# Second attention of a two-layer kernel: products of scores in bursts of three tiles, and a fixed order on TensorE

## Chip, cores and metric

The kernel runs on one core of one Trainium2 chip. The metric is the device time of one execution in microseconds (us); lower is better. One chip core has a matrix engine (TensorE, "PE" in the profile, with its weight loads as "PEld"), a vector engine (VectorE, "DVE"), an activation engine (ScalarE, "ACT"), a general engine (GpSimd, "POOL") and SyncE ("SP"), which starts transfers here. Each engine takes its instructions in the order of its own queue.

## The reference

Two layers, each an attention and a mixture of experts, on 4 sequences of 1024 tokens of 256 numbers in fp32. The change lies in the second attention:

```python
Q = x @ wq + bq                      # x is the normalised input, (4, 1024, 256)
K = x @ wk + bk
V = x @ wv + bv
Q = Q.reshape(B * H, S, D)           # 64 heads of 1024 rows of 16 numbers
...
scores = jnp.einsum('bqd,bkd->bqk', Q, K) / jnp.sqrt(jnp.float32(D))
attn = jax.nn.softmax(scores, axis=-1)
ctx = jnp.einsum('bqk,bkd->bqd', attn, V)
...
out = ctx @ wo + bo
out = out + x
out = (out - mu) * jax.lax.rsqrt(var + LN_EPS) * gamma + beta
```

There is no mask: every one of the 64 heads has a full 1024 x 1024 table of scores. The softmax is computed with the true maximum of each row taken off before the exponential.

## The kernel before

**How the second attention is tiled.** The 64 heads are taken in 32 pairs (`NP`), numbered `p`. One pair of heads gives the 128 rows of one output tile of tokens. The table of scores of a pair is computed twice. First with queries down and keys across (`maxima`, L1368): VectorE reduces each 128 x 1024 tile to row maxima (L1381). Then with keys down and queries across (`scores`, L1407): here two more small products take the row maxima off (the operand `top_st`), and ScalarE writes the exponentials to the tile `pT` (L1424), which the weighted sums (`sums`, L1427) use with the values `v_t` as weights. Both kinds of score tile lie in PSUM under the tag `two`, of which there are three (`psa`, L80). The sums of a pair gather in one PSUM bank, `acc`. Everything else that passes through PSUM there uses one bank, `misc`.

**The loop.** A step `s` stands for one of eight blocks of keys (`KT`) of one pair; it has two halves, so a pair has 16 half-steps and the stage 512. In a half-step the loop (L1605) records, in this order: one tile of `scores` (two products with the keys, L1416, then two with the maxima, L1416), one tile of `maxima` for the pair that comes 12 steps later (`AHEAD`; two products, L1374), one half of the sums of the step before (four products, L1431), and then `some`, which advances the side jobs by one piece. The two products of a kind in a score tile use the two halves of the array's rows, 64 each, one head per half; the four products of the sums use four groups of 32 output columns.

**Side jobs.** `some` (L1567) takes one piece each from `between` and `aside`, and one from `outs`, `projects` or `gating`; `sort` follows when there was little else. They are generators:
- `outs` holds `put_out` (L1442) for a finished pair. Its first piece transposes the copy `oT` of the sums (L1447) and divides (L1452, L1454); later ones transpose again (L1464), project (L1470) and add the residual, in which VectorE's L1477 needs GpSimd's addition of `bo` (L1476).
- `projects` holds `project` (L1269: L1286, and L1296 with two PSUM tiles of tag `two`) and `values` (L1323: L1336), once each for four pairs.
- `between` and `gating` hold the layer norm after the attention (`finish`: L1492 to L1509), and the first steps of the next mixture of experts (L958 to L996).
- `sort` ranks tokens for the experts of the first half of the batch on VectorE, and `aside` then writes those ranks by 16 scatters (L1542) on GpSimd.

When all eight blocks of a pair have their maxima, `max_rows` (L1383) reduces once more, transposes the result on TensorE (L1390), splits it in two parts, and sends it through DRAM into a row buffer of `top_ring` by four transfers on SP (L1398, L1403).

**What sets the order.** The engines' queues are filled by a scheduler at build time. It goes by the recorded order and by its own estimate of when each instruction can start, so it may put a later instruction ahead of an earlier one. `issue_after` forbids this for what is recorded inside it: side jobs are held behind the newest instruction of the main work on their engine, kept in the dictionary `newest`. For TensorE `newest` holds only the last of the sums; score products and the transpose of the tops are free to move.

Of the kernel before, what the change touches and what calls it, by code (L numbers as in the profile page):

```python
# [18 lines left out]
P = 128  # L19
# [4 lines left out]
UT = 4  # L24
UN = UT * P
NU = NT // UT
# [13 lines left out]
def two_layers(  # L40
# [33 lines left out]
    nc = tc.nc  # L74
    mm = nc.tensor.matmul
# [1121 lines left out]
    with ExitStack() as lc:  # L1197
# [68 lines left out]
        halves, vals, normed = {}, {}, {}  # L1266
        newest = {}

        def project(u: int):  # L1269

            xnT = normed[u] = pool.tile([P, 2, UN], F32, tag="xnT", name="xnT_a1", bufs=1)
            for jp in range(UT // 2):
                xns = []
                for i in (u * UT + 2 * jp, u * UT + 2 * jp + 1):
                    xn = work.tile([P, D], F32, tag="xn", name="xn")
                    nc.gpsimd.tensor_scalar(
                        xn, x_t[i], mv_all[:, i, 0:1], rstd_all[:, i : i + 1],
                        ALU.subtract, ALU.mult,
                    )
# [88 lines left out]
        def maxima(p: int, j: int, kk: int, tops):  # L1368

            q_st, k_st = q_ring[p % RING], k_ring[p % RING]  # L1370
            sc = two_banks().rearrange("p (h c) -> p h c", h=2)
            for hh in range(2):
                rows = slice(HR * hh, HR * hh + HR)
                mm(  # L1374
                    sc[:, hh],
                    lhsT=q_st[rows, j * P : (j + 1) * P],
                    rhs=k_st[rows, kk * 512 : (kk + 1) * 512],
                    start=True,
                    stop=True,
                )  # L1380
            newest["vector"] = nc.vector.tensor_reduce(tops[:, :, j, kk], sc, AX.X, ALU.max).ins  # L1381

        def max_rows(p: int, tops):  # L1383

            top = small.tile([P, 2 * 8], F32, tag="top", name="top")
            nc.vector.tensor_reduce(
                top, tops.rearrange("p h j k -> p (h j) k"), AX.X, ALU.max
            )
            ps = misc_bank()
            nc.tensor.transpose(ps[:16, :P], top, ident)  # L1390
            split = pool.tile([16, 2, P], F32R, tag="top_split", name="top_split")
            nc.scalar.copy(split[:, 0, :], ps[:16, :P])
            nc.vector.tensor_tensor(
                split[:, 1, :], ps[:16, :P], split[:, 0, :].bitcast(F32), ALU.subtract
            )
            d = dram.tile([2, 2, S], F32, tag="tops_d", name="tops_d", bufs=3)
            for hh in range(2):
                nc.sync.dma_start(  # L1398
                    out=d[hh].rearrange("n (j q) -> j n q", q=P),
                    in_=split[8 * hh : 8 * hh + 8].bitcast(F32),  # L1400
                )
            for hh in range(2):
                nc.sync.dma_start(  # L1403
                    out=top_ring[p % 2][HR * hh : HR * hh + 2].bitcast(F32), in_=d[hh]
                )

        def scores(p: int, k: int, rp: int):  # L1407


            q_st, k_st = q_ring[p % RING], k_ring[p % RING]  # L1410
            sc = two_banks()
            cols = slice(rp * 512, (rp + 1) * 512)
            for top in range(2):
                for hh in range(2):
                    rows = slice(HR * hh, HR * hh + HR)
                    mm(  # L1416
                        sc[:, hh * 512 : (hh + 1) * 512],
                        lhsT=minus[rows] if top else k_st[rows, k * P : (k + 1) * P],
                        rhs=(top_ring[p % 2] if top else q_st)[rows, cols],
                        start=not top,  # L1420
                        stop=bool(top),
                    )
            pt = pool.tile([P, 1024], F32, tag="pT", name="pT", bufs=6)
            newest["scalar"] = nc.scalar.activation(pt, sc, AF.Exp).ins  # L1424
            return pt

        def sums(p: int, k: int, hh: int, pts, oT_ps):  # L1427

            n = 2 * p + hh
            for r in range(4):  # L1430
                newest["tensor"] = mm(  # L1431
                    oT_ps[32 * r : 32 * r + 32, hh * D : (hh + 1) * D],
                    lhsT=vals[n // HU][:, n % HU, k, :],
                    rhs=pts[r // 2][:, hh * 512 + (r % 2) * D : hh * 512 + (r % 2 + 1) * D],
                    start=(k == 0 and hh == 0),
                    stop=(k == 7),
                    skip_group_check=True,
                ).ins

        ys = []  # L1440

# [109 lines left out]

        AHEAD = 12
        KT = 8
        outs, projects, between, gating, sort, aside = [], [], [], [], [], []
# [20 lines left out]
        def all_of(jobs):  # L1577
            while jobs:
                step(jobs)

        top_parts = {}

        def maxima_step(m: int, kk: int):
            p, j = divmod(m, KT)
# [16 lines left out]
        for m in range(AHEAD):  # L1601
            for kk in range(2):
                maxima_step(m, kk)
        before, oT_ps = None, None
        for s in range(NP * KT + 1):  # L1605
            p, k = divmod(s, KT)
            if k == 0:
                if p % UT == 1:

                    all_of(projects)  # L1610
                    if p // UT + 1 < NU:
                        projects.append(values(p // UT + 1))
                if p + 3 < NP:
                    load(p + 3)
                if p % UT == 3 and p + 5 < NP:
                    all_of(projects)
                    projects.append(project(p // UT + 2))
            if k == 1:
# [10 lines left out]
            if k == 0 and s:  # L1629
# [5 lines left out]
                outs.append(put_out(p - 1, oT))  # L1635
# [102 lines left out]
```

## Time and profile before

| what | us |
|---|---|
| median of 3 runs (2560.59 to 2582.25) | 2569.44 |
| the profiled execution, own time | 2580.51 |
| its span in the trace | 2578.6 |
| TensorE busy (90% of the span) | 2328.3 |
| VectorE busy (54%) | 1396.7 |
| ScalarE busy (38%) | 986.0 |
| GpSimd busy (25%) | 640.4 |
| row maxima L1381, 512 instructions, mean 1.217 | 619.0 |
| exponentials L1424, 512, mean 1.025 | 523.5 |
| weighted sums L1431, 4096 records | 345.0 |
| keys' products L1416, 1024 | 261.2 |
| maxima's products L1374, 1024 | 232.1 |
| subtracted maxima L1416, 1024 | 208.2 |

Busy times are shares of an average over quite different stages; the second attention is one of them. TensorE's records overlap, since products in different parts of the array run side by side and ends are modelled, so its busy time says little about how fast it could go. Distances from start to start in the timeline say more. An fp32 product of the sums leaves two records, so that four products show as eight.

The busy time of each engine in three stretches of the stage (columns: engine, busy us in a window of 100 us):

| window | PE | DVE | ACT | granted clock |
|---|---|---|---|---|
| 1650 to 1750 | 97.47 | 77.78 | 66.86 | 1.00 |
| 1950 to 2050 | 97.48 | 75.58 | 62.79 | 0.98 |
| 2150 to 2250 | 93.59 | 93.52 | 64.82 | 1.00 |

### The profile page before, as it was taken

Reading aid. Unit: us, or ns where it says so; the run is one execution under the profiler, and the core shown is the slowest. Engines: PE = TensorE matmul, PEld = TensorE weight load, DVE = VectorE, ACT = ScalarE, POOL = GpSimd, SP = SyncE. Lnnn points to the kernel's source line nnn. Section 1 sums busy time; section 2 is a strip of 40 time slices with the busy share of each in tenths; the row PEclk is TensorE's granted clock in tenths of the full one; section 3 lists DMA queues with packets and bytes.
Section 4 is the critical chain, followed back from the end, with each engine's and each line's share of the span. In section 5 each row is a group of like instructions: output and inputs, shape, how many; then the busy total and the mean of one; then the engine's idle time right before and its main releaser. Section 6 shows DMA issues by size and latency. Waiting matters only on the chain.

```text
span 2578.6 us, 42321 instructions
## 1 busy us (share of the span) xinstructions
PE 2328.3 (90%) x16882; PEld 1389.6 (54%) x16882; DVE 1396.7 (54%) x2272; ACT 986.0 (38%) x1345; POOL 640.4 (25%) x741
## 2 busy tenths in 40 slices
PE   6999999899999999999957999999999999997534
PEld 3566666566578888885533444444444444443322
DVE  6445445514222222224536777676767798994293
ACT  1333333221122222221112666565656565665311
POOL 2333333601700000004340013122221211124354
PEclk8998999899999999999976999999999999998667
DMA  3000000510266666663143231312131312100134
GB/s 92 17 10 10 10 13 8 166 48 23 104 185 196 194 192 194 194 192 88 51 98 68 52 74 52 67 43 68 43 68 43 67 43 67 43 19 11 54 118 131
DMA packets 202976, 207.52 MB, mean 80 GB/s; under 512 B 89128, under 2 KB 163496, under 8 KB 202780
## 3 DMA queue, kind: packets, MB, share of 16 engines
q1 hardware_dynamic: 179292, 163.37, 23.4%
q0 software_dynamic: 11792, 30.18, 3.9%
q10 hardware_dynamic: 11696, 11.27, 1.3%
q8 instruction: 133, 2.18, 0.4%
q14 instruction: 63, 0.52, 0.1%
HBM read 141.49 MB, written 58.80 MB: 78 GB/s over the span
## 4 chain that ended last, share of the span: by engine, by line
PE 72%; DVE 15%; ACT 4%; issue 4%; DMA 2%; POOL 2%; SPq 0%; POOLq 0%; ACTq 0%; DVEq 0%
PE two L847 10%; PE two L1416 10%; PE acc L1431 8%; PE two L643 7%; DVE tops L1381 6%; PE two L329 5%; PE two L1374 4%; PE acc L871 4%; PE two L258 2%; PE two L1296 2%; PE misc L660 2%; PE acc L660 2%; PE two L321 2%; PE acc L396 1%; DVE glu_b L860 1%
## 5 line engine op out<-in xcount | busy, mean ns | idle before, releaser
L1381 DVE TENSOR_REDUCE tops<-two 128x2 f32<-128x1024 f32 x512 | 619.0, 1217 | 126.7 <-PE two L1374 124.7
L1424 ACT ACTIVATE pT<-two 128x1024 f32<-128x1024 f32 x512 | 523.5, 1025 | 329.1 <-PE two L1416 324.5
L1431 PE MATMUL acc<-pT,v_t 128*32 128x256 f32 x4096 | 345.0, 397 | 5.4 <-ACT pT L1424 5.4
L1416 PE MATMUL two<-q_st,k_st 64*128 64x512 f32 x1024 | 261.2, 503 | 32.2 <-DVE tops L1381 19.7
L847 PE MATMUL two<-xbT,w_t 128*128 128x256 f32 x1248 | 275.8, 379 | 0.7 <-ACT xbT L839 0.7
L847 PEld LDWEIGHTS two<-xbT,w_t 128*128 128x128 f32 x1248 | 237.0, 190 | 33.1 <-ACT xbT L839 0.9
L1374 PE MATMUL two<-k_st,q_st 64*128 64x512 f32 x1024 | 232.1, 421 | 20.1 <-DMA k_st<-halves 9.3
L643 PE MATMUL two<-xnT_f,w_t 128*128 128x512 f32 x512 | 229.8, 601 | 3.1 <-DVE glu L652 3.1
L1416 PEld LDWEIGHTS two<-q_st,k_st 64*128 64x128 f32 x1024 | 97.2, 185 | 225.0 <-issue 127.9
L860 DVE SCALAR_TENSOR_TENSOR glu_b<-two,b_blk,act_b 128x256 f32<-128x256 f32 x156 | 75.3, 483 | 249.4 <-ACT act_b L857 249.4
L1416 PE MATMUL two<-top_st,minus 64*128 64x512 f32 x1024 | 208.2, 401 | 0.0
L857 ACT ACTIVATE act_b<-two,b_blk 128x256 f32<-128x256 f32 x156 | 74.0, 474 | 330.6 <-PE two L847 287.6
L898 POOL DMA_INDIRECT yr<-ys_d,slot x64 | 61.4, 960 | 538.1 <-DMA ys_d<-yb 471.1
L1431 PEld LDWEIGHTS acc<-pT,v_t 128*32 128x32 f32 x4096 | 86.8, 108 | 167.9 <-issue 145.8
L871 PE MATMUL acc<-w_t,glu_b 128*128 128x256 f32 x624 | 161.8, 392 | 6.4
L1374 PEld LDWEIGHTS two<-k_st,q_st 64*128 64x128 f32 x1024 | 107.6, 191 | 92.4 <-DVE tops L1381 28.9
L643 PEld LDWEIGHTS two<-xnT_f,w_t 128*128 128x128 f32 x512 | 96.3, 192 | 111.7 <-issue 105.7
L355 DVE TENSOR_REDUCE top<-two 128x4 f32<-128x768 f32 (+1 forms) x128 | 112.5, 919 | 71.3 <-PE two L329 71.3
L381 POOL TENSOR_SCALAR_AFFINE_SELECT pT<-pT 128x1024 f32<-128x1024 f32 x64 | 70.4, 1100 | 305.5 <-ACT pT L378 305.5
L378 ACT ACTIVATE pT<-two 128x768 f32<-128x768 f32 (+1 forms) x128 | 93.7, 783 | 121.2 <-PE two L329 120.7
L651 ACT ACTIVATE act<-two,bT 128x512 f32<-128x512 f32 x64 | 44.0, 687 | 241.8 <-PE two L643 230.7
L871 PEld LDWEIGHTS acc<-w_t,glu_b 128*128 128x128 f32 x624 | 112.2, 189 | 37.5 <-DVE glu_b L860 25.2
(304 smaller groups left out, 3110.9 us busy)
## 6 DMA issues: line engine op xcount, KB each, us to landing
w_t<-in_L_ffn_rw_dram SPq DMA_DIRECT2D x117, 512.0 KB
halves<-split SPq DMA_DIRECT2D x64, 256.0 KB
q_st<-halves SPq DMA_DIRECT2D x128, 128.0 KB
k_st<-halves SPq DMA_DIRECT2D x256, 64.0 KB
xs_d<-zeros SPq DMA_DIRECT2D x6, 1664.0 KB
xb<-xs_d SPq DMA_DIRECT2D x39, 256.0 KB
ys_d<-yb ACTq DMA_DIRECT2D x39, 256.0 KB
b_t<-in_L_ffn_rb_dram SPq DMA_DIRECT2D x39, 128.0 KB
```

Source lines behind the costliest of these rows:

```text
L329: mm(parts[r][:, gg, :], lhsT=left[32 * r : 32 * r + rows, g, l0 : l0 + P], rhs=right[32 * r : 32 * r + rows, g, r0 : r0 + n], start=(mask ...
L355: nc.vector.tensor_reduce(tops[i][:, 2 * ab : 2 * ab + 2, 2 * gp : 2 * gp + 2], scs[ab], AX.X, ALU.max)
L643: mm(ps[:, n * 512 : (n + 1) * 512], lhsT=w_t[:, kc, f * P : (f + 1) * P], rhs=xnT[:, kc, cols], start=(kc == 0), stop=(kc == 1),)
L660: mm(ps[:, jj * D : (jj + 1) * D], lhsT=glu[:, f, j * P : (j + 1) * P], rhs=w3_t[:, f, :], start=(f == 0), stop=(f == NF - 1),)
L847: mm(ps[:, (2 * m + ff) * BT : (2 * m + ff + 1) * BT], lhsT=w_t[:, kc, f * P : (f + 1) * P], rhs=xbT[:, kc, :], start=(kc == 0), stop=(kc ...
L860: nc.vector.scalar_tensor_tensor(glu[:, f, :], ps[:, (2 + ff) * BT : (3 + ff) * BT], b_blk[1][:, f, n : n + 1], act, ALU.add, ALU.mult,)
L871: mm(ps[:, a * D : (a + 1) * D], lhsT=glu[:, f, a * P : (a + 1) * P], rhs=w3_t[:, f, :], start=(f == 0), stop=(f == NF - 1),)
L1374: mm(sc[:, hh], lhsT=q_st[rows, j * P : (j + 1) * P], rhs=k_st[rows, kk * 512 : (kk + 1) * 512], start=True, stop=True,)
L1381: newest["vector"] = nc.vector.tensor_reduce(tops[:, :, j, kk], sc, AX.X, ALU.max).ins
L1416: mm(sc[:, hh * 512 : (hh + 1) * 512], lhsT=minus[rows] if top else k_st[rows, k * P : (k + 1) * P], rhs=(top_ring[p % 2] if top else q_st ...
L1424: newest["scalar"] = nc.scalar.activation(pt, sc, AF.Exp).ins
L1431: newest["tensor"] = mm(oT_ps[32 * r : 32 * r + 32, hh * D : (hh + 1) * D], lhsT=vals[n // HU][:, n % HU, k, :], rhs=pts[r // 2][:, hh * 5 ...
```

## The change

The loop over steps becomes a loop over half-steps `h`, and the work of a half-step is cut into `weigh` (the score tile whose exponentials are wanted), `seek` (the maxima tile), `add_up` (the sums) and `rest` (side jobs). Three half-steps are recorded together: `weigh`, `seek`, `weigh`, then one half of the sums, then `seek`, `weigh`, `seek`, then two halves of the sums. The last half-step but one of each pair, and the first two of all, stay by themselves. A new function `own` holds every product of scores and sums behind the one recorded before it on TensorE, and the transpose of the tops is held in the same way. `max_rows` is no longer called in the middle of the maxima but from `rest`, after the sums. The sum's copy `oT` and `put_out` now start right after the last sums of a pair, before the pieces of `rest`; before, one `some` came first.

```diff
+        def own(*a, **k):
+            with ExitStack() as behind:
+                if "tensor" in newest:
+                    behind.enter_context(tc.issue_after(newest["tensor"]))
+                newest["tensor"] = mm(*a, **k).ins
...
-                mm(
+                own(
                     sc[:, hh],
...
-            nc.tensor.transpose(ps[:16, :P], top, ident)
+            with ExitStack() as behind:
+                if "tensor" in newest:
+                    behind.enter_context(tc.issue_after(newest["tensor"]))
+                newest["tensor"] = nc.tensor.transpose(ps[:16, :P], top, ident).ins
...
             if j == KT - 1 and kk == 1:
-                max_rows(p, top_parts.pop(p))
+                full.append(p)
...
-            pts = []
-            for half in range(2):
-                if p < NP:
-                    pts.append(scores(p, k, half))
-                    maxima_step(s + AHEAD, half)
-                if s:
-                    sums(*divmod(s - 1, KT), half, before, oT_ps)
-                some(half == 0 and k % 4 == 0)
-            before = pts
...
+        def rest(*hs):
+            while full:
+                p = full.pop(0)
+                max_rows(p, top_parts.pop(p))
+            for h in hs:
+                some(h % 8 == 0)
+        h = 0
+        while h < LAST:
+            if h < 2 or h % (2 * KT) == 2 * KT - 2 or h + 3 > LAST:
+                weigh(h)
+                seek(h)
+                add_up(h)
+                rest(h)
+                h += 1
+            else:
+                weigh(h)
+                seek(h)
+                weigh(h + 1)
+                add_up(h)
+                rest(h)
+                seek(h + 1)
+                weigh(h + 2)
+                seek(h + 2)
+                add_up(h + 1)
+                add_up(h + 2)
+                rest(h + 1, h + 2)
+                h += 3
```

`weigh` also calls `turn` at the first half-step of a pair, which loads the queries and keys of the pair three further on and starts `project` and `values`, as the head of the old step did.

More of the change, by code (lines that the diff above doesn't have):

```diff
@@ L1415, in scores @@
                     rows = slice(HR * hh, HR * hh + HR)
-                    mm(
+                    own(
                         sc[:, hh * 512 : (hh + 1) * 512],
@@ L1430, in sums @@
             for r in range(4):
-                newest["tensor"] = mm(
+                own(
                     oT_ps[32 * r : 32 * r + 32, hh * D : (hh + 1) * D],
@@ L1437, in sums @@
                     skip_group_check=True,
-                ).ins
+                )
         ys = []
@@ L1579, in all_of @@
                 step(jobs)
-        top_parts = {}
+        top_parts, full = {}, []
         def maxima_step(m: int, kk: int):
@@ L1603, in two_layers, with turn, weigh, seek @@
                 maxima_step(m, kk)
[L1604 to L1618, printed above, removed]
-                oT_ps = acc_bank()
-            pts = []
-            for half in range(2):
-                if p < NP:
-                    pts.append(scores(p, k, half))
-                    maxima_step(s + AHEAD, half)
-                if s:
-                    sums(*divmod(s - 1, KT), half, before, oT_ps)
-                some(half == 0 and k % 4 == 0)
-            before = pts
-            if k == 0 and s:
+                while full:
+                    p = full.pop(0)
+                    max_rows(p, top_parts.pop(p))
+        weights, oT_ps = {}, None
+        LAST = 2 * NP * KT + 2
+        def turn(p: int):
+            if p % UT == 1:
+                all_of(projects)
+                if p // UT + 1 < NU:
+                    projects.append(values(p // UT + 1))
+            if p + 3 < NP:
+                load(p + 3)
+            if p % UT == 3 and p + 5 < NP:
+                all_of(projects)
+                projects.append(project(p // UT + 2))
+        def weigh(h: int):
+            if h % (2 * KT) == 0:
+                turn(h // (2 * KT))
+            st, half = divmod(h, 2)
+            if st < NP * KT:
+                weights[h] = scores(*divmod(st, KT), half)
+        def seek(h: int):
+            st, half = divmod(h, 2)
+            maxima_step(st + AHEAD, half)
+        def add_up(h: int):
+            nonlocal oT_ps
+            st, hh = divmod(h, 2)
+            if not 1 <= st <= NP * KT:
+                return
+            p, k = divmod(st - 1, KT)
+            if k == 0 and hh == 0:
+                oT_ps = acc_bank()
+            sums(p, k, hh, [weights[2 * st - 2], weights[2 * st - 1]], oT_ps)
+            if k == KT - 1 and hh == 1:
                 oT = work.tile([P, 4, 2, HN], F32, tag="oT", name="oT1", bufs=2)
@@ L1634, in two_layers @@
                 )
-                outs.append(put_out(p - 1, oT))
+                outs.append(put_out(p, oT))
+        def rest(*hs):
+            while full:
+                p = full.pop(0)
+                max_rows(p, top_parts.pop(p))
+            for h in hs:
[21 more added lines that the diff above has]
+                h += 3
         all_of(outs)
```

## The prediction

> **What bounds the kernel now.** I read the page's forty slices first, to find the stage that the diff touches, then the timeline inside that stage, then the waits.
>
> ```profile
> PE   6999999899999999999957999999999999997534
> ...
> DVE  6445445514222222224536777676767798994293
> ...
> PEclk8998999899999999999976999999999999998667
> ```
>
> A slice is 64.5 us. The second attention fills slices 22 to 37: its first product of scores starts at 1382.8 us and its last at 2405.7. TensorE (PE) is full there and VectorE (DVE) is at 7, but in the last third at 8 and 9. The timeline shows one half-step between 1601 and 1604 (columns: start, duration, engine, line, operation):
>
> ```profile
> 1601.74 0.64 PE L1431 MATMUL acc<-pT,v_t 128*32 128x256 f32 x8
> ...
> 1602.31 0.49 PE L1416 MATMUL two<-q_st,k_st 64*128 64x512 f32 x2
> ...
> 1602.64 0.40 PE L1416 MATMUL two<-top_st,minus 64*128 64x512 f32 x2
> 1602.88 0.39 PE L1374 MATMUL two<-k_st,q_st 64*128 64x512 f32 x2
> 1603.17 1.02 ACT L1424 ACTIVATE pT<-two 128x1024 f32<-128x1024 f32 x1 [0.48 <-PE two L1416]
> 1603.20 0.64 PE L1431 MATMUL acc<-pT,v_t 128*32 128x256 f32 x8
> 1603.31 1.23 DVE L1381 TENSOR_REDUCE tops<-two 128x2 f32<-128x1024 f32 x1 [0.24 <-PE two L1374]
> ```
>
> Call the pairs K (L1416 keys), T (L1416 tops), M (L1374) and the sums S. Durations overlap, so I read start to start: S to K 0.57, K to T 0.33, T to M 0.24, M to S 0.32; medians over the stage 0.569, 0.337, 0.234, 0.326, together **1.466** a half-step. Equal pairs are not equally long: the first after S and the last before S take 0.10 and 0.09 more than the one between. ACT and DVE show gaps, PE none: PE bounds. A clean pair of heads (16 half-steps) takes 26.25 us by the starts of T: 23.5, plus 2.2 for its output's and top's transposes and projection, plus 0.55 explained below. One place is different. Waits of 2336 to 2366 and the timeline:
>
> ```profile
> 2341.73 1.12 POOL L1542 DMA_INDIRECT rank_d<-place,at_i  x1 [23.00 <-DVE at_i L1539]
> ...
> 2360.85 0.96 POOL L1542 DMA_INDIRECT rank_d<-place,at_i  x1 [0.30 <-issue]
> 2361.83 0.73 POOL L1476 TENSOR_TENSOR y<-y,rows_b 128x256 f32<-128x256 f32 x1
> 2362.60 0.42 DVE L1477 TENSOR_TENSOR y<-y,misc 128x256 f32<-128x256 f32 x1 [14.32 <-POOL y L1476]
> 2362.94 2.35 DVE L1381 TENSOR_REDUCE tops<-two 128x2 f32<-128x1024 f32 x2
> 2364.21 0.79 PE L1416 MATMUL two<-q_st,k_st 64*128 64x512 f32 x2 [11.68 <-DVE tops L1381]
> ```
>
> Sixteen scatters stand on POOL ahead of one small add; DVE waits for that add, the maxima behind it wait too, and PE stands 11.7 us.
>
> **What the Trainium skill says.** "TensorEngine Tiling (Array Packing)", section Key Properties: changing the tiling mode drains TensorE. The trace agrees: scores are 64*128 pairs, sums 128*32, and the pairs beside a change are the long ones. "Perfetto Trace Analysis", Optimization Strategy: a gap that repeats on the engine that should be full can mean that there is no room in PSUM for the next tile. The trace of before hardly shows this (PE waited 6.7 us for maxima between 1450 and 2350). "ScalarE: Activation LUTs", What ACT_TABLE_LOAD costs: about 1.28 us a load; here 1.28 too, and two with their square root hold ACT 2.9 us.
>
> **The change, part by part.** I took the order of both built programs as the map and these times as prices.
>
> *Bursts.* Of each 16 half-steps, 15 become five triples: K T M K T | S | M K T M | S S, and one stays single. A triple has two bursts in place of three, and two S rounds together. Its length without waits: (0.337+3x0.234+0.326) + 0.569 + (0.337+2x0.234+0.326) + S S. Two rounds: where the old order put ten records of sums together (five products, two rounds) the next product starts 1.01 later; I take 1.0. Sum 4.065. M to K inside a burst is never seen; bounds 0.225 (the shortest K to T, the same shape) and 0.337 (the first of a burst); I take 0.234, the neighbour T to M.
> Waits: all three `two` tiles are used by one burst. By the timeline ACT starts 0.49 after T's start and takes 1.025 (next may start 0.115 before the end), DVE 0.43 after M and takes 1.19 (0.085), and PE goes on 0.05 after the tile is read. From 0: exp of the first tile ends 1.85, so the second burst's M may start at 1.90; PE comes at 1.93. First maxima end 2.19, K may start 2.25, PE comes 2.27. Second exp ends 2.76; the last M may start 2.81, PE comes 2.74: **wait 0.075**. All else is later. Triple 4.14 against 3x1.466 = 4.40: -0.262 each, 160 of them: **-41.9**.
>
> *Order pinned.* The old order split sums five and three products 16 times: 1.01+0.56 against 2x0.569, 0.42 each: **-6.7**. It stood the first T behind nothing: products for later tiles passed it while its rows came by DMA (1382.8 to 1388.9). Pinned, they queue behind it, but the transpose of the tops comes two products earlier (2x1.13): 0, bounds -3 to +3.
>
> *The stall on POOL.* In the new build the scatters come after the adds of all remaining tiles, and their index after the last maxima: **-11.7**. Their 20 us then stand before the last tiles' normalising (L965) and DVE's reading of the ranks before the last tile's output. The old tail needs 57 us from the last maxima to the last tile's L1504; counting the new queue (index some 19 after the maxima, 16x1.26, the read, then the old tail's steps) I get about 61: **+4**, bounds -6 to +16.
>
> *Tops.* `max_rows` moves behind the sums, its transpose directly behind S S of the burst that holds the last maxima. That M starts at 2.81, DVE is free for it at 3.47, ends 4.67, `top` 0.17: PE may go on at 4.88 where it would at 4.14: 0.74 a pair of heads. Before, the transpose split M (0.476+0.207+0.427 against 0.326+0.206): 0.58 in 23 pairs, 0.43 in 9. 32x0.74-17.2 = **+6.5**. The rows' four DMAs on SP go with it; ten half-steps of lead (15 us) hide them, and no wait of PE for them shows in mid-stage; without that cover T would wait. Loads in `turn` keep their place.
>
> *Jobs inside a burst.* The output's transposes (L1447) stood at a border of S in all cases; now 31 times after the next K T. They wait for the copy of `oT`: S S ends 1.28 after its first start for ACT, copy 0.58, against PE's K T 0.57: 0.365, plus two more mode changes, 0.2: 31x0.565 = **+17.5** (bounds 6 and 25). Of other jobs 46 fall inside (before 14, tops apart); 29 split a pair, which I price by the split of M, 0.5; 17 cost 0.2; less the old 2.8: **+15** (5 to 25). Where a job lies in a triple the 0.075 is covered: 77 times, **-6**.
>
> *ACT and DVE.* Table loads: 16 pairs of them; the half beside the `oT` copy cost 1.1 as before (PE waited 1.04 at 1671.8), the half in a triple's third exp have 0.96 of slack for 2.9: 1.0 more, **+8** (0 to 16). DVE's other work in 1450 to 2350 is 714-556 = 158 us. A K had 0.6 of slack to its maxima; in a triple DVE has 0.44 free before the first reduction and none before the second K. Half-covered batch-norm steps give **+5** (0 to 50, see C).
>
> Sum: -41.9-6.7-11.7+4+6.5+17.5+15-6+8+5 = **-10**. The profiled execution (2580.5, span 2578.6) lies 11 above the median shown, 2569.4; differences carry over: **2560**.
>
> **Rivals.** *A, likeliest (0.50):* the above, own range 2535 to 2590. For it: PE is full, so a saved change is saved time; against full gain: three tiles for bursts of three. *B (0.22):* jobs and ACT cost nothing extra, since waits cover each other: -41.9-6.7-11.7+6.5 = -54: 2516. *C, slower (0.18):* lockstep. DVE's 158 us of other work stand in front of a burst's first maxima and the second K waits. Slices of 8 and 9 on DVE speak for it, the mean of 7 against. It decides from 16 us (a tenth of the work) on; at a third, 53 instead of 5, +38: 2607. *D (0.10):* it doesn't do what it says: the long first and last pairs belong to their own weights, not to the change of mode, and a burst saves nothing. Then 0.075 on 83 triples is +6, the jobs lose 9.6 of switching: 6-6.7-11.7+4+6.5+11.3+11.6+8+5 = +34: 2603. The order of the build excludes that the bursts aren't there: 158 double and 190 single groups of sums.
>
> **How the numbers follow.** One per cent is 25.7 us, about what a measurement tells from no change: faster is under 2544, slower over 2595. Faster: B 0.22 and 0.08 of A, 0.30. Same: 0.42 of A, 0.05 of C, 0.03 of D, 0.50. Slower: 0.13 of C, 0.07 of D, 0.20. From 2516 to 2604 leaves out half of B's and half of C's and D's.
>
> **What would show it.** T to M, M to K near 0.234 and a plain triple near 4.14 (else D); PE's waits for `pT` at the last M about 0.08, not 0.3; PE waiting about 0.7 for `top` once in each pair of heads; waits of PE for DVE's maxima under 20 us (C if over 40); no 11.7 us gap. The forecast is wrong if PE waits for reductions in most triples, or the tail after the last maxima grows by over 15.

## The result, and the profile after

The changed kernel takes **2585.47 us** (median of 20 runs, 2577.03 to 2599.38), the kernel before in 20 runs 2576.80: a ratio of **1.0043, interval 1.0029 to 1.0057**, slower by 11 us by this ratio and by 8.7 by the two medians. That is within one per cent and inside the range, on the other side of zero from the forecast of 10 us less.

The profiled execution happens to be the fastest of the changed kernel (span 2575.2). Everything ahead of the second attention was 14 us shorter in it by chance: its first product of the maxima starts at 1338.9, against 1353.0 before. From there to the end it takes 1236.3, before 1225.6: 10.7 us more, which agrees with the ratio. So the two traces can be compared from that point on. The forty slices of the changed kernel's page:

```profile
PE   7999999899999999999958999999999998999434
...
DVE  5445444415222222225437767676767787987293
...
PEclk8999998899999999999978999999999999999667
```

At this scale nothing has happened: TensorE still reads 9 through the stage (8 in one slice), VectorE 6 to 9, the granted clock 9. The loss is too thinly spread to show in tenths of a slice. The timeline of the changed kernel, from the last triple of a pair of heads (all products and sums are now L1274, since `own` issues them; the maxima's reduction is L1388, `top` is L1393, its transpose L1400):

```profile
1639.79 1.22 DVE L1388 TENSOR_REDUCE tops<-two 128x2 f32<-128x1024 f32 x1
...
1640.48 0.50 PE L1274 MATMUL two<-k_st,q_st 64*128 64x512 f32 x2
...
1641.06 0.19 PEld L1274 LDWEIGHTS two<-q_st,k_st 64*128 64x128 f32 x2 [0.40 <-DVE tops L1388]
1641.07 0.50 PE L1274 MATMUL two<-q_st,k_st 64*128 64x512 f32 x2
1641.17 0.19 PEld L1274 LDWEIGHTS two<-top_st,minus 64*128 64x128 f32 x2
...
1641.40 0.40 PE L1274 MATMUL two<-top_st,minus 64*128 64x512 f32 x2
1641.41 0.19 PEld L1274 LDWEIGHTS two<-k_st,q_st 64*128 64x128 f32 x2
1641.48 2.32 DVE L1388 TENSOR_REDUCE tops<-two 128x2 f32<-128x1024 f32 x2
1641.64 0.39 PE L1274 MATMUL two<-k_st,q_st 64*128 64x512 f32 x2
...
1641.96 1.07 PE L1274 MATMUL acc<-pT,v_t 128*32 128x256 f32 x16
1643.71 0.42 DVE L1502 BATCH_NORM_STATS2 st<-y 128x6 f32<-128x256 f32 x1
1644.05 0.17 DVE L1393 TENSOR_REDUCE top<-tops 128x16 f32<-128x32 f32 x1
...
1644.27 0.28 PE L1400 MATMUL misc<-ident,top 128*16 128x128 f32 x1 [1.24 <-DVE top L1393]
...
1644.48 0.50 PE L1274 MATMUL two<-q_st,k_st 64*128 64x512 f32 x2
```

Three things are to be seen.
- **The burst's gain is there.** T at 1641.40 to M at 1641.64 is 0.24, and the sums of two halves, begun at 1641.96, would free PE some 1.0 later.
- **K waits for a reduction, and pays twice.** M starts at 1640.48; its K should follow 0.34 later, but the tile that it writes is freed by the reduction that ends at 1641.01. K starts at 1641.07, 0.25 late, and then takes 0.33 to T instead of the 0.23 of a pair inside a burst. In pairs of heads 0 to 29 I find 95 such K behind the M that opens a second burst: 72 of them late by 0.16 on the mean, and the K that came late have a median of 0.337 to T, the others 0.232. The weight loads (PEld) show where the second payment comes from: those of M stand 0.23 ahead of it (1641.41 for 1641.64), while those of the late K begin only with K itself (1641.06); T's begin at 1641.17, and T starts 0.23 behind them. Over all K behind an M in these pairs the loads of the late ones start with the product, those of the others 0.23 ahead of it (medians).
- **PE waits for `top`.** A batch norm stands between the last maxima and `top` on VectorE, and the transposition, held in its place, starts at 1644.27, 2.31 after the sums began where 1.0 was needed. PE's next products stand behind it.

The waits of PE in the stage, 1450 to 2350 us (columns: what waited, for what, us in total, times, longest):

```profile
PEld two L1274 <- DVE tops L1388: 68.3, 170, 1.4
...
PE misc L1400 <- DVE top L1393: 29.7, 28, 3.1
...
PE two L1274 <- DVE tops L1388: 14.4, 27, 1.0
...
PE two L1274 <- ACT pT L1434: 6.6, 9, 0.9
```

Before, these were 37.4 in 75 waits for the weight loads (28.1 for K and 9.3 for M), 3.0, 6.7 and 11.7. The 6.7 is all that the prediction read of them; the 37.4 of the weight loads stood in the same view. A weight load that waits is partly covered by the product in front of it, so I add up starts instead. For each group of equal products I take the undisturbed distance to the next one (0.234, 0.10 more for the first and 0.09 more for the last of a burst, 0.57 and 1.0 for the sums, the shortest one seen for a side job), call it PE's own work, and put what is above it to the wait of the group that follows:

| us | before, pairs 0-29 | after | difference |
|---|---|---|---|
| changes of mode (first and last of a burst) | 91.8 | 70.7 | -21.1 |
| sums | 281.8 | 251.0 | -30.8 |
| pairs split by a side job | 17.0 | 12.4 | -4.6 |
| products, side jobs | 506.4 | 507.5 | +1.1 |
| waits of K | 23.4 | 39.4 | +16.0 |
| T late after K | 1.5 | 14.3 | +12.8 |
| waits of M | 6.3 | 14.5 | +8.2 |
| waits of the sums | 4.5 | 9.7 | +5.2 |
| waits of the tops' transpose | 3.9 | 33.3 | +29.4 |
| waits of other side jobs | 7.6 | 17.0 | +9.4 |

PE's own work fell by 55.4, and 81.0 of waits came instead; by the starts of T, pairs 0 to 29 took 947.7 before and 971.1 after. The rest: from the first M to the first T 35.9 became 31.7; pair 30, which had held the stall on POOL, 43.2 became 28.0; from the start of pair 31 to the end 198.7 became 205.5.

### The profile page after: what moved, and what is told of

It reads as the page before. It is cut to its first block, busy times and chain, and to the rows that moved or that the text cites. A ratio compares the mean times of both kernels' runs of the same rounds, so it can differ in the third digit from the quotient of the medians.

```text
span 2575.2 us, 42345 instructions
## 1 busy us (share of the span) xinstructions
PE 2292.2 (89%) x16882; PEld 1402.5 (54%) x16882; DVE 1388.7 (54%) x2272; ACT 979.6 (38%) x1345; POOL 640.9 (25%) x741
## 4 chain that ended last, share of the span: by engine, by line
PE 67%; DVE 20%; ACT 5%; issue 3%; DMA 3%; POOL 2%; SPq 0%; POOLq 0%; ACTq 0%; DVEq 0%
PE two L1274 12%; PE two L847 10%; DVE tops L1388 9%; PE two L643 7%; PE acc L1274 6%; PE two L329 5%; PE acc L871 4%; PE two L258 2%; PE two L1303 2%; PE misc L660 2%; PE acc L660 2%; PE two L321 2%; ACT pT L1434 2%; PE acc L396 1%; PE misc L440 1%
## 5 line engine op out<-in xcount | busy, mean ns | idle before, releaser
L1388 DVE TENSOR_REDUCE tops<-two 128x2 f32<-128x1024 f32 x512 | 610.4, 1218 | 131.0 <-PE two L1274 129.5
L1434 ACT ACTIVATE pT<-two 128x1024 f32<-128x1024 f32 x512 | 512.3, 1024 | 285.5 <-PE two L1274 280.9
L1274 PE MATMUL acc<-pT,v_t 128*32 128x256 f32 x4096 | 305.4, 392 | 9.1 <-ACT pT L1434 9.1
L1274 PE MATMUL two<-k_st,q_st 64*128 64x512 f32 x1024 | 249.3, 466 | 23.9 <-DVE tops L1388 12.3
L1274 PE MATMUL two<-q_st,k_st 64*128 64x512 f32 x1024 | 243.2, 464 | 18.3 <-DVE tops L1388 9.9
L1274 PE MATMUL two<-top_st,minus 64*128 64x512 f32 x1024 | 217.8, 401 | 0.0
L1274 PEld LDWEIGHTS acc<-pT,v_t 128*32 128x32 f32 x4096 | 99.5, 109 | 161.2 <-issue 115.5
L1274 PEld LDWEIGHTS two<-k_st,q_st 64*128 64x128 f32 x1024 | 104.6, 192 | 136.3 <-ACT pT L1434 47.6
L1274 PEld LDWEIGHTS two<-q_st,k_st 64*128 64x128 f32 x1024 | 98.6, 186 | 127.2 <-DVE tops L1388 62.4
L355 DVE TENSOR_REDUCE top<-two 128x4 f32<-128x768 f32 (+1 forms) x128 | 112.6, 920 | 68.3 <-PE two L329 68.2
L1486 POOL TENSOR_TENSOR y<-y,rows_b 128x256 f32<-128x256 f32 x32 | 23.4, 733 | 481.5 <-DVE y L1483 481.5
```

The lines of the kernel that those rows point to most:

```text
L355: nc.vector.tensor_reduce(tops[i][:, 2 * ab : 2 * ab + 2, 2 * gp : 2 * gp + 2], scs[ab], AX.X, ALU.max)
L1274: newest["tensor"] = mm(*a, **k).ins
```

## The experiments

Ratios are to the kernel before, run beside each on the same chip. Two speeds of chip were met: the kernel before takes 2574 to 2577 us on some, 2640 to 2645 on others. Stage times agree (pairs 0 to 19: 631.6 and, in a kernel with the same order there, 631.1), since the difference lies ahead of the second attention: its first product of the maxima starts at 1335 to 1354 us on the ones, at 1398 to 1418 on the others. Where two kernels are set against each other below, differences of medians and of ratios can differ by some 5 us; where it matters both are given.

**Tops late.** The changed kernel; the reduction to `top` stays where it is, the transposition and what follows it come one piece of side jobs later.

```diff
+            return top
+
+        def send_rows(p: int, top):
+
             ps = misc_bank()
...
+            while reduced:
+                send_rows(*reduced.pop(0))
             while full:
                 p = full.pop(0)
-                max_rows(p, top_parts.pop(p))
+                reduced.append((p, max_rows(p, top_parts.pop(p))))
```

> The changed kernel, but the transpose of a pair's row maxima is issued one border of sums later than the small reduction it waits for. Theory 1 (the transposes pinned straight behind the sums stall TensorE): the waits before them, some 33 us in the changed kernel, fall under 3 us, and the time falls by 25 to 32 us, to a ratio of about 0.993 to before. Theory 2 (TensorE and VectorE run in lockstep, so VectorE would be late elsewhere): TensorE's waits for the maxima's tiles grow by most of that and the ratio stays at 1.000 to 1.004.

Measured **0.9872 (0.9836 to 0.9908)**, 2546.38 us: 39 below the changed kernel by medians, 44 by the ratios, where 25 to 32 were expected. The same place of its timeline, in the same pair of heads:

```profile
1644.85 1.07 PE L1274 MATMUL acc<-pT,v_t 128*32 128x256 f32 x16
...
1645.85 0.50 PE L1274 MATMUL two<-q_st,k_st 64*128 64x512 f32 x2
...
1646.94 0.17 DVE L1393 TENSOR_REDUCE top<-tops 128x16 f32<-128x32 f32 x1
...
1647.41 0.64 PE L1274 MATMUL acc<-pT,v_t 128*32 128x256 f32 x8
...
1647.98 0.28 PE L1404 MATMUL misc<-ident,top 128*16 128x128 f32 x1
```

The products follow the sums after 1.00; `top` is as late as ever (1646.94), but its transposition comes behind another half of the sums and waits for nothing. In pairs 0 to 30 the waits of the tops go from 34.5 to 0.0 and the 31 pairs take 42.6 less (999.1 to 956.5), so the wait did not come back elsewhere; the remaining 8 are smaller waits of jobs and sums. The waits of K stayed (43.6 in pairs 0 to 29, T 12.8). The same kernel once more, beside later ones:

> The changed kernel with the tops' transposition one piece of side jobs later, once more, as the mark for the first run on the same chip. Expected as measured before: 0.984 to 0.991.

0.9862 (0.9833 to 0.9892).

**Tops free.** The changed kernel with `issue_after` taken from the tops' transposition alone.

> The changed kernel, with only the pin on the transpose of the tops taken away; the scheduler then puts it inside a burst, after a pair K T or between the two products of one pair. Theory 1: the wait for the small reduction shrinks to under 10 us of 33, but each transpose inside a burst costs two changes of mode, 0.2, or 0.5 where it splits a pair, some 10 us; ratio 0.997. Theory 2: 1.002 to 1.004.

Measured 1.0005 (0.9987 to 1.0023), 4.6 us below the changed kernel by medians and 10 by the ratios, where 18 were expected. The waits of side jobs, tops among them, in pairs 0 to 29 fell from 50.3 to 21.1, but the cost of pairs split by a job went from 12.4 to 25.2, and the sums waited 5.2 more. Freed, the transposition goes into the middle of a pair of products in 21 of 30 cases, and stands between T and M in 7 others. What the tops need is a later place, not a free one.

**Outputs late.** The changed kernel with `put_out` handed on one piece later, so that its transpositions meet a finished `oT`.

```diff
-                outs.append(put_out(p, oT))
+                ready.append(put_out(p, oT))
...
             for h in hs:
                 some(h % 8 == 0)
+            outs.extend(ready)
+            ready.clear()
```

> The changed kernel, but a finished pair's output job starts one border of sums later, so that its transposes find their input ready; in the built order nearly all side jobs then stand at borders of sums (3 split pairs in place of 29). Theory 3 (jobs inside bursts are a main loss): the time falls by 15 to 30 us, ratio 0.993 to 0.999, and split pairs, waits before jobs and mode changes shrink. Rival (theory 1 alone): less than 8 us, ratio 1.001 to 1.004.

Measured 1.0057 (1.0042 to 1.0073): no gain. Its trace says why. In pairs 0 to 19 splits fell from 6.6 to 0, changes of mode by 2.0 and waits of jobs other than tops from 10.6 to 5.6, but waits of tops rose by 3.3 and of K, T and M by 5.6; 5.7 were left. In pairs 20 to 29 the tops' waits rose from 13.7 to 23.3. And the ranks' index came early again, ahead of the last maxima: the stall on POOL was back, pair 30 took 40.5 instead of 28.0.

**Both.** Tops and outputs late together.

> Both of the two edits, tops late and output late. If theories 1 and 3 both hold and add up: 40 to 60 us less than the changed kernel, ratio 0.981 to 0.989. If the losses are one and the same slack (lockstep with VectorE): no better than the better one of the two alone.

> Tops and outputs moved, once more, as the mark for the second run on one chip: as measured before, 0.982 to 0.989.

0.9855 (0.9827 to 0.9883) and 0.9876 (0.9850 to 0.9901), the same as with the tops alone. The number lies in the range forecast for two gains that add up, but the tops alone give it. Pairs 0 to 19 gained 8.6 on it (613.0 against 621.6), 5.2 were lost in the next ten, pair 30 lost 12.8 to the stall, and what follows it was 7 shorter. The stall in the timeline:

```profile
2316.57 0.42 DVE L1491 TENSOR_TENSOR y<-y,misc 128x256 f32<-128x256 f32 x1 [12.05 <-POOL y L1490]
2316.91 2.35 DVE L1388 TENSOR_REDUCE tops<-two 128x2 f32<-128x1024 f32 x2
```

As in the kernel before, DVE waits for a small addition behind 13 scatters on POOL, with the maxima behind it.

**The order alone.** The kernel before with `own` on products and sums; no bursts, tops as before.

> The kernel before, with only the pin of the products and sums added (no bursts, tops free). The prediction's term: 16 groups of five and three sums become four and four, 0.42 each, 7 us less; ratio 0.997. If pinning makes TensorE wait for late inputs that it formerly passed: 1.000 or above.

Measured 0.9972 (0.9957 to 0.9987), as expected, but not for the reason given. Against a kernel with the old order on that chip, the sums took 7.6 less in pairs 0 to 29 (the predicted 6.7), and the waits of K 7.6 more; the pairs together took 3.4 more (954.0 against 950.6). The gain that the two traces show is the opening, 30.2 from the first M to the first T against 36.1. From the first M to the end they differ by 3.3 only; the rest of the measured 8 stays open.

**The stall on POOL, four times.** First the kernel before, with the scatters taken from `some`, so that they are recorded after the loop.

> The kernel before, with the 16 scatters of ranks recorded after the loop in place of among its last side jobs. The prediction's terms: the stall of 11.7 us goes, the tail after the last maxima grows by 4 (-6 to +16): 8 us less, ratio 0.997. Rival: the scatters' 20 us stand in the tail in full: 0 to 8 us more, ratio 1.000 to 1.003.

0.9997 (0.9981 to 1.0014), which tells nothing of the stall: the scheduler put the scatters where they had been, 24.2 us ahead of the end of the last maxima (before: 23.6), and pair 30 still took 43.2. So in the next the index is held as well, behind the last maxima; in the one after it the scatters are held behind POOL's additions of tile 29, which is where the changed kernel has them; and in the last one POOL's small addition is put behind 4 of the 16 scatters.

```diff
                 step(between)
-                step(aside)
...
             for jobs in (between, gating, sort, aside):
-                step(jobs)
+                with ExitStack() as behind:
+                    if jobs is aside:
+                        behind.enter_context(tc.issue_after(newest["vector"]))
+                    step(jobs)
```

> The kernel before with nothing but the ranks' index and its 16 scatters held behind the last maxima; this is the stall of the prediction by itself. Theory (as predicted, -11.7 and +4): pair of heads 30 falls from 43 us to 28 to 31, the tail grows by 4 to 8, ratio 0.996 to 0.998. Rival (it comes back whole): 0.999 to 1.001.

> The kernel before with nothing but the index and the scatters at that same place on POOL. Theory (-11.7 and +4 of the prediction): pair of heads 30 falls from 43 to 28, the time from the last maxima to the end grows by 4 to 8; ratio 0.9958 to 0.9975. Rival (all of it comes back in the tail, as with the scatters right behind the last maxima): 0.999 to 1.002.

> The kernel before with the small addition on POOL that DVE waits for put behind 4 of the 16 scatters, not behind all 16; the ranks come as early as before. Theory (the stall is a matter of the queue's order, and its 11.7 us can be had): pair of heads 30 falls from 43 us to 29 to 32, the time from the last maxima to the end stays within 3 us, ratio 0.9945 to 0.9965. Rival (POOL's 20 us of scatters are on the path wherever they stand): 0.998 to 1.002.

| the kernel before, scatters | ratio | pair 30 | pair 31 to the end |
|---|---|---|---|
| as they are | 1 | 43.2 | 198.7 |
| recorded last, placed as before | 0.9997 (0.9981 to 1.0014) | 43.2 | 201.4 |
| right behind the last maxima | 1.0020 (1.0005 to 1.0035) | 29.0 | 218.8 |
| at the changed kernel's place on POOL | 1.0008 (0.9992 to 1.0024) | 29.0 | 217.4 |
| addition behind 4 of the 16 | 0.9983 (0.9967 to 1.0000) | 36.5 | 207.6 |

Each time that pair 30 gained, what follows it took most or more of it back. The waits in the tail (2335 to 2405) of the fourth row:

```profile
DVE key L1143 <- DMA rank<-rank_d: 21.7, 1, 21.7
...
PE misc L989 <- DVE y L1477: 15.0, 1, 15.0
```

The ranks are read back from DRAM (L1178) after the last scatter. VectorE's first use of them (L1143) waits 21.7 us and has an output's addition (L1477) behind it, and a gating product of TensorE (L989), ahead of the last sums, waits for the bank that this addition frees. Three in-order queues hand one delay on. The changed kernel has the same order on POOL but another on VectorE (timeline):

```profile
2402.19 0.23 DVE L1143 TENSOR_SCALAR key<-rank 128x128 f32<-128x128 f32 x1 [10.15 <-DMA rank<-rank_d]
...
2415.32 0.42 DVE L1487 TENSOR_TENSOR y<-y,misc 128x256 f32<-128x256 f32 x1 [3.38 <-PE misc L1480]
```

Its last sums had ended at 2402.0, so the wait of 10.15 held none of them up, and the tail grew by 6.8 only. What the prediction claimed for the stall is right for this kernel, but it isn't a property of the scatters' place.

The same three edits (behind the last maxima, at the changed kernel's place, behind 4 of the 16) in the kernel with tops and outputs late:

> Both moves of the tops and of the outputs, and now the ranks' index and its 16 scatters held behind the last maxima. In the kernel with both moves the stall on POOL was back: its pair of heads 30 took 39.5 us, against 26.7 with the tops alone moved. Theory (the stall's return hid what the outputs' move gained): pair 30 falls to 27, the tail behind the last maxima grows by 4 to 8, the ratio to before goes from 0.9855 to about 0.982 (0.980 to 0.984). Rival (what the stall cost comes back whole in the tail): 0.985 to 0.987.

> Tops and outputs moved, and the ranks' index and 16 scatters on POOL at the place where the changed kernel has them (behind the additions of all but the last two tiles). Theory: pair of heads 30 takes 27 us (39.5 with both moves alone), the time from the last maxima to the end grows from 210 to about 216; ratio 0.982 to 0.985, 4 to 12 us below the third of these runs. Rival (the outputs' move brings nothing): within 0.002 of the third.

> The same edit in the kernel with tops and outputs moved. Theory: pair of heads 30 falls from 39.5 to 27 to 29, 9 to 12 us below the third of these runs. Rival: within 4 us of it.

0.9923 (0.9894 to 0.9953), 0.9905 (0.9876 to 0.9933) and 0.9906 (0.9888 to 0.9923): none better than the kernel with the stall. Pair 30 fell from 39.5 to 27.7, 28.3 and 33.8, and from pair 31 to the end, 197.3 with the stall, they took 225.3, 216.6 and 208.0.

**Bursts alone.** The first and the second of the last three kernels, without bursts: each half-step by itself, all else equal.

```diff
-            if h < 2 or h % (2 * KT) == 2 * KT - 2 or h + 3 > LAST:
+            if True:
```

> The first of these three with every half-step by itself (scores, maxima, one half of the sums, side jobs), so with no bursts; all else, the pinned order, the tops and outputs moved and the scatters held, is the same. Theory (in pairs of heads 0 to 29 bursts save 55 us of mode changes and sums and cost 37 of waits for the score tiles): slower than the first by 15 to 20 us, 0.988 to 0.991 to before. Rival (DVE's waits eat the bursts whole, and what was gained came from the order and the moved jobs): within 0.002 of the first.

> The first of these runs without bursts, every half-step by itself. Theory (bursts save 49 us of mode changes and sums in pairs of heads 0 to 29, and cost 42 of waits for score tiles): slower than the first by 5 to 11 us, 0.002 to 0.0045 in the ratio. Rival (the pair of runs with the disturbed tail understated the bursts): slower by 15 to 20 us, 0.006 to 0.008.

0.9945 (0.9927 to 0.9963) against 0.9923 with bursts, and 0.9936 (0.9907 to 0.9965) against 0.9905 (2561.02 and 2550.42 us): by medians 5.7 us where 15 to 20 were expected, and 10.6 where 5 to 11 were. Intervals overlap; the traces of the second pair are clearer: pairs 0 to 29 take 936.4 without and 922.8 with bursts (933.2 and 924.2 in the first). Without bursts PE's own work is 50.8 more, and the waits are 37.0 less. PE's waits for the maxima, 1450 to 2300, without bursts and then with them:

```profile
PEld two L1274 <- DVE tops L1388: 37.2, 75, 1.4
```

```profile
PEld two L1274 <- DVE tops L1388: 80.8, 167, 1.9
```

By the starts of all K, T and M, they lose 80.8 instead of 41.4 (K 17.0, T 11.3, M 11.1 more). So here the bursts are worth their saved modes and sums, less three quarters of that in waits.

**Half the maxima.** To see whether VectorE is behind those waits: the reduction reads only the first 256 of 512 columns of each head (0.69 us instead of 1.2), in the changed kernel and in the kernel before.

```diff
-nc.vector.tensor_reduce(tops[:, :, j, kk], sc, AX.X, ALU.max)
+nc.vector.tensor_reduce(tops[:, :, j, kk], sc[:, :, :256], AX.X, ALU.max)
```

> The changed kernel with the row maxima taken over half of each tile's columns (the other half is left out, so the row maxima subtracted are lower): the reduction takes about 0.7 in place of 1.22. If waits for VectorE inside the triples cost as the trace of the changed kernel says (a plain triple near 4.25 in place of 4.06), triples fall to 4.06 to 4.10 and the tops' stall to about 0.3: 45 to 60 us less than the changed kernel, ratio 0.980 to 0.987. If VectorE's reductions are not what holds the triples: only the tops' stall shrinks, 15 to 20 us, ratio 0.996 to 0.998.

> The control: the kernel before with the same half of the row maxima left out. TensorE hardly waits for them there: 5 to 15 us less, ratio 0.994 to 0.998. If VectorE holds the old loop too: as much as in the changed kernel.

0.9789 (0.9752 to 0.9825) and 0.9832 (0.9794 to 0.9870). The control missed its expectation by far: the 24 maxima tiles ahead of the loop gave 12.4 (first M to first T 23.7), and pairs 0 to 30 gave 26.2, much of it where the ranking works on VectorE. The difference between the two still answers. With whole maxima the changed kernel's pairs 0 to 30 take 999.1 against 990.9; with half, 938.3 against 967.6. In pairs 0 to 29 of the changed kernel the waits of K fell from 39.4 to 21.1, T's lateness from 14.3 to 2.6, and waits of all side jobs, tops among them, from 50.3 to 20.5, while M's, which wait for exponentials, rose from 14.5 to 16.2. So most of the tops' loss, and the long waits of K, are VectorE's.

The plain triple, one without a side job, says something else. There are 60 of them in pairs 0 to 29 of either trace. In the changed kernel they take 4.27 in the median and 4.25 at the shortest; with half the maxima, where 4.06 to 4.10 was expected, still 4.26 and 4.25. K is on time now, but the last M is not (timeline with half the maxima, end of a triple that began at 1604.54):

```profile
1607.03 0.40 PE L1274 MATMUL two<-top_st,minus 64*128 64x512 f32 x2
1607.36 0.19 PEld L1274 LDWEIGHTS two<-k_st,q_st 64*128 64x128 f32 x2 [0.37 <-ACT pT L1434]
1607.36 0.50 PE L1274 MATMUL two<-k_st,q_st 64*128 64x512 f32 x2
...
1607.79 1.07 PE L1274 MATMUL acc<-pT,v_t 128*32 128x256 f32 x16
```

M waits 0.10 for the exponential that reads its score tile, its weights are loaded no sooner than it starts, and the sums follow 0.43 after it instead of 0.33. In the changed kernel K's short waits in the second burst take up the same time, so that in a plain triple relieving VectorE wins back the long waits alone (mean 4.44, with half the maxima 4.28).

## Why the prediction was wrong, step by step

Its terms, put together as the traces can show them (PE's own work: -41.9 and -6.7, without the 160 waits of 0.075, 12.0, and with the old tops' splits, -17.2, and the jobs' mode changes and splits, +6.2 and +15; from its own figures the saving of a triple is 0.258, not 0.262, which makes -41.9 into -41.3 and changes nothing):

| us | predicted | measured |
|---|---|---|
| opening | 0 | -4.2 |
| PE's own work | -56.6 | -55.4 |
| waits of M for exponentials | +6 | +8.2 |
| **K and T, for VectorE's reductions** | **+5** | **+28.8** |
| tops | +23.7 | +29.4 |
| `oT` and other jobs' waits | +11.3 | +9.4 |
| table loads, waits of the sums | +8 | +5.2 |
| pair 30 | -11.7 | -15.2 |
| pair 31 to the end | +4 | +6.8 |
| sum | -10 | +13, or +10.7 with 2 at the edges of pairs that this count misses |

- **Right: the bursts' own price.** T to M and M to K inside a burst have a median of 0.23, two halves of sums take 1.00. Rival D is out. "TensorEngine Tiling (Array Packing)", Key Properties, says only that a change of mode drains TensorE; the trace gave the price, and it carried over to an order not yet seen.
- **Wrong: "Half-covered batch-norm steps give +5".** This is the step that failed: it measured 28.8, more than the whole forecast gain of 10. The working had PE coming to the second burst's K at 2.27 when it might start at 2.25, and called that no wait. A margin of 0.02 isn't cover: 72 of 95 such K came late, and in first bursts 37 of 110 K came late, by 0.42 on the mean. Each late one paid 0.10 more to its T; this had no term at all and makes 12.8 of the 28.8. With VectorE on time the triple would still have missed its 4.14, since the "wait 0.075" of the last M for its exponential lacked the same 0.10: the 60 plain triples of pairs 0 to 29 took 4.25 at the shortest and 4.44 on the mean, 18 us more than forecast in these alone. The trace of before had the price of a late product: of its 440 M between a T and a group of sums 31 came late, and their median to the sums is 0.43, that of the others 0.33. Rival C had VectorE's part of the mechanism and set its threshold by VectorE's share; the measured waits of K and T lie between its mild and its full case. Its sign, over 40 us of waits for maxima, is met only if the weight loads' waits are counted, 68.3, which the prediction had not read in before either.
- **Mis-sized: tops.** The mechanism is as predicted (PE waits behind the pinned transposition, once a pair of heads), the size 0.98 more than before for each of 30 pairs, instead of 0.74. The forecast has the transposition 1.74 after the sums began, and where the reductions came on time it stands there (1.71 to 1.85 in 12 of 30 pairs); with a batch norm ahead of `top` it came at 2.31, as shown above, and with the ranking on VectorE at up to 4.1. It is also the loss that a change of order won back: tops late gave 39 us by medians.
- **Right in this kernel, wrong as a rule: the stall.** Pair 30 and the tail together gave -8.4, predicted -7.7. But at the same place on POOL in the kernel before, the tail took all of it (1.0008). And pair 30 gave 15.2 where the stall was priced at 11.7, since the stall also slowed what came behind it. In the trace of before the granted clock (windows, third number from the end) is at half when PE starts again at 2364.21, and full only from about 2369.8:

```profile
2364.00:2367.00 3.00, 2.79 (x10) 0.96 (x13) 3.00 (x10) 1.25 (x2) 1.03 (x1) 0.50 0.19 11
2367.00:2370.00 3.00, 3.00 (x20) 0.87 (x16) 2.78 (x13) 1.03 (x2) 2.95 (x5) 0.53 0.14 42
```

  K to T takes 0.59 there instead of 0.34. If all of these 5.6 us were stretched like that, 2.4 of them are lost (an estimate), which is most of the missing 3.5.
- **Right number, wrong reason: the pinned order.** -6.7 by the sums is about what they gave, and K's waits took it; the opening, priced at 0, gave 5.9 in the traces, and the rest of the 8 measured is not shown.
- "Perfetto Trace Analysis", Optimization Strategy, names a gap that repeats on the full engine as a sign of too little room for the next tile. The prediction found hardly one in the trace of before, as it left out the weight loads, which waited 75 times; in the changed kernel they wait 170 times. Three score tiles hold one burst, so a burst can go no faster than VectorE and ScalarE free them. More tiles were not tried.

The likeliest way to beat both kernels is the changed one with its tops one piece later (0.9872 and 0.9862); outputs late beside it brings no more that shows (0.9855 and 0.9876). Still open is how to have both that and pair 30: it would need the index, the scatters, L1143 and the last outputs ordered together, and that wasn't tried.

## What to carry to other kernels

When products are gathered into bursts to save changes of mode, work out when each tile of the burst comes free, and count a margin smaller than the other work of the freeing engine as a wait. Price a wait, however short, with the lost head start of the weight loads on top (0.10 us here), and read the waits of the weight loads along with those of the products. An instruction pinned in the queue of the bounding engine must have its input ready; if it comes from an engine with a backlog, put it one piece of work later, don't unpin it. A stall taken away in front of a chain of in-order queues is a gain only if the end of that chain is seen to come earlier.

## What the runs showed of the hardware

- A pair of products that had to wait takes 0.34 to the next, like the first of a burst, not 0.23, even without a change of mode. In the traces the weights of an undisturbed pair are loaded 0.23 ahead of it, those of a late one only as it starts.
- After a long idle time TensorE is slow for some microseconds. "TensorE: Matmul & The Clock Gate", What's actually happening, says that its clock is halved after an idle window of about 3.4 us and full again after at least one busy window of that length. In the kernel with both moves and the scatters behind the last maxima, PE stood still for 17.3 us, until 2420.65 (windows; the granted clock is the third number from the end of a line):

```profile
2415.00:2420.00 5.00, 0.00 (x0) 0.00 (x0) 1.07 (x6) 0.00 (x0) 0.53 (x1) 0.50 0.12 7
2420.00:2424.00 4.00, 3.35 (x12) 2.01 (x14) 1.55 (x9) 1.60 (x3) 0.00 (x0) 0.50 0.00 0
2424.00:2428.00 4.00, 4.00 (x20) 1.68 (x16) 0.32 (x1) 1.30 (x3) 0.00 (x0) 0.56 0.00 0
2428.00:2432.00 4.00, 4.00 (x46) 2.31 (x42) 0.71 (x3) 2.95 (x3) 0.00 (x0) 1.00 0.00 0
```

  The half clock lasts some 7 us after work began again (0.56 in the third line means half until about 2427.5), twice the shortest time that the page allows, and the sums' eight records took 1.08 there instead of 0.64. Behind the stall of 11.7 us in the kernel before it was 5.6 us. By the same stretching, an estimate, such stalls cost 2 to 3 us more than themselves.
- The two kinds of chip differ by some 65 us in the kernel before, and the mean granted clock from 600 to 900 us, ahead of the second attention, is 1.00 on the ones and 0.89 to 0.90 on the others in the profiles taken; from 1450 to 2100 us it is 0.98 to 1.00 on both.
